# Cross-attention's borders: first queries ahead of the token transposes, folded weights between the first maxima, biases as bf16 rows

## The chip, the cores and the metric

The program runs on one core of one Trainium2 chip, as one launch. The metric is the device time of an execution in microseconds (us), the median over several runs. The profile is of one execution, and it has its own time.

## The reference, cut to what matters

The model holds x as 2 batches of 256 tokens with 256 channels and runs six layers, each added to x: a gelu layer against the context, a latent attention, a mixture-of-experts FFN ("MoE"), then a cross-attention, a holographic attention and a mixture attention. The change touches the cross-attention and what it hands to the holographic attention:

```python
def _L1_xattn_ref(values, keys, queries, mask, w_out, b_out):   # 16 heads of 16, 4096 keys
    energy = jnp.einsum('nqhd,nkhd->nhqk', q, k)
    energy = jnp.where(mask == 0, jnp.float32(-1e+20), energy)
    attn = jax.nn.softmax(energy / math.sqrt(EMBED), axis=3)
    out = jnp.einsum('nhql,nlhd->nqhd', attn, v).reshape(N, q_len, HEADS * HEAD_DIM)
    return out @ w_out.T + b_out

def _L1_attn_ref(x, Wq, bq, Wk, bk, Wv, bv):
    # unit_projection: fft, divided by its magnitude; bind/unbind: products of spectra
    query = unit_projection(jnp.einsum('bsd,ed->bse', x, Wq) + bq)
    keys = unit_projection(jnp.einsum('bsd,ed->bse', x, Wk) + bk)
    values = unit_projection(jnp.einsum('bsd,ed->bse', x, Wv) + bv)
    s = jnp.cumsum(bind(keys, values), axis=1)
    return unbind(s, query)

x = x + _L1_xattn_ref(ctx_1024, ctx_1024, _layernorm(x), mask, w_out, b_out)
x = x + _L1_attn_ref(_layernorm(x), Wq, bq, Wk, bk, Wv, bv)
```

## The kernel before, in words

Tokens lie on the partitions: x is four tiles (`NT`) of 128 tokens by 256 channels. A layernorm (`layernorm_T`) takes means and variances, makes the normalised tiles `xn` on VectorE (L121), transposes them with eight 128x128 transposes (`transpose_tokens`, L135), and two copies out of PSUM (L44 on VectorE, L46 on ScalarE) give `xnT`, channels on partitions.

**From the MoE.** Its results are gathered by eight indirect DMAs on POOL into the tiles `G` (L838), which VectorE adds to x (L807). Buffers opened after the MoE take over its memory, so their loads wait until the MoE is through with it.

**Cross-attention.** Its work is 32 units, one for each batch and head, with 8 steps each. A unit has its keys in one of five buffers `keys0` to `keys4`: four groups of 32 partitions, each with 16 rows of transposed context (`load_keys`, L868, SP) and 16 rows of ones (`set_ones`, L875; once for each buffer). Against the ones stand rows of the query tile `q0` that carry the negated maximum of each query, so that the energies come out with the maximum subtracted. Thus every unit is walked over twice: first step by step for maxima (`max_mms`: four f32 matmul records per step at L939 into `pm`, one VectorE maximum at L960), then for energies (`pe`), exponentials on ScalarE (L1055), masks on POOL (L1061) or VectorE, and the value products (`pav`). `place_mm` (L939) issues nearly all of these matmuls. A loop over T runs the maxima `LEAD` = 12 steps ahead of the energies. The stretch in which only maxima run is called the lead here. After eight maxima of a unit, `reduce_max_of` (mneg L967, mrows L969) and two transfers on SP, through `maxd` in HBM, bring the maxima into the query tile. `transfers` issues these and the later units' keys and queries in the order written.

Ahead of the lead come, in program order: loads of keys0 and keys1 with their ones, the output weights `wo` and bias `bo`, the layernorm "d", the queries of unit 1 by DMA, the ones of the three other key buffers, and the weights of the holographic attention (`wq`, `bq`, `dft`, `gates`, L914 to L918, SP). The queries of unit 0 don't go through DMA: `pad` (L926) puts the first 16 channels in place, sixteen matmul records at L930 place them, and L934 copies them to `q0`. After the eighth maximum, four VectorE additions put `bo` into x (L1164).

**Tail.** After the last step come 12 transposes of `wq` (L1178) with two copies (L1181), `combine` for the last unit (division by the sum, L1023 to L1028), the token transposes, and the output projection (L1189, added to x at L1192). Then the holographic weights are multiplied by the DFT matrix ("folded"): L1208 for the weights, L1216 for the biases, copies L1212 and L1219. The layernorm "e" follows. `spectrum` multiplies xnT by the folded weights `WD` (L1253), and adds the folded bias through a product of a tile of ones and `bD`, whose first row alone is not zero (L1257). Products and magnitudes on ScalarE, POOL and VectorE follow, and then the last layer.

Instructions on an engine run in its own order; `keep_in_program_order`, `issue_after` and manual dependencies fix parts of that order, and a scheduler decides the rest. DMAs are issued by SP, ACT and POOL, and a DMA also waits for the one before it on its lane.

Of the kernel before, what the change touches and what calls it, by code (L numbers as in the profile page):

```python
# [9 lines left out]
F32 = mybir.dt.float32  # L10
# [16 lines left out]
def tile_perceiver(ctx: ExitStack, tc: tile.TileContext, t):  # L27
# [67 lines left out]

    def layernorm_stats(mv, sm, tt):
        st = sm.tile([P, 6], F32, name="st", bufs=2)
        nc.vector.bn_stats(st, x[:, tt, :])
        nc.vector.bn_aggr(mv[:, tt, :], st)

    def layernorm_T(es, tag, scale_rows=None, mv=None, then=None, between=None, turn=None):
# [3 lines left out]
        pt, name = turn or (pool(es, f"lnp_{tag}", 2, PSUM), "ps_t")  # L105
# [14 lines left out]
        for tt in range(NT):  # L120
# [3 lines left out]
            )  # L124
        if between is not None:
            between()
        transpose_tokens(pt, xnT, xn, name)
# [419 lines left out]
    with ExitStack() as es:  # L547
# [246 lines left out]
        for n, u in enumerate(work):  # L794
# [8 lines left out]
            if u == ("s", 3):  # L803
                with tc.issue_after(turned_last[0].ins):
                    for tt in range(NT):
                        for i in range(2):
                            nc.vector.scalar_tensor_tensor(  # L807
# [44 lines left out]
    sig = wh.tile([P, 16], F32, name="sig")  # L852
    with ExitStack() as es:
# [19 lines left out]
        def set_ones(i, queues):  # L873
            for g in range(4):
                queues[g % len(queues)].dma_start(  # L875
# [4 lines left out]
        for u in range(2):  # L880
            list(load_keys(u))
            set_ones(u, (nc.sync, nc.gpsimd) if u == 0 else (nc.gpsimd,))
# [6 lines left out]
        QN = 5  # L889
        q0 = wk.tile([P, QN, S], F32, name="q0")  # L890
        with ExitStack() as es1:
            rooted = layernorm_T(es1, "d", scale_rows=anyq, mv=mvd, then=AF.Exp)

# [14 lines left out]
        with tc.issue_after(rooted.ins):  # L908
            nc.scalar.mul(q0[:, 1:, :], ones[:, 0:1].unsqueeze(2).to_broadcast([P, QN - 1, S]), 0.0)
        list(load_queries(1, (nc.sync, nc.scalar)))  # L910
        for i in range(2, KEYS):
            set_ones(i, (nc.gpsimd,))
        for j, n in enumerate("qkv"):
            nc.sync.dma_start(wq[:, j], t[f"W{n}T"].rearrange("(k p) e -> p k e", p=P))  # L914
            with nc.allow_non_contiguous_dma(reason="biases by channel"):
                nc.sync.dma_start(bq[:, j, :], t[f"L1_attn_b{n}"].rearrange("(k p) -> p k", p=P))
        nc.sync.dma_start(dft, t["dft"].rearrange("(k p) e -> p k e", p=P))
        nc.sync.dma_start(gates, t["L1_ffn_gates"].partition_broadcast(P))  # L918
# [3 lines left out]
        LEAD = 12  # L922
        mxs, max_rows = {}, {}


        nc.vector.tensor_copy(pad[:, :, 0:16], xn[:, 0:2, 0:16])  # L926
        pt = p_s.tile([P, 2, 512], F32, name="pm")[:, 0, 0:S]
        for qb in range(2):
            for g in range(4):
                nc.tensor.matmul(  # L930
                    pt[32 * g : 32 * g + 32, qb * P : (qb + 1) * P], lhsT=pad[:, qb, :], rhs=ident,
                    start=True, stop=True,
                )
        nc.vector.tensor_copy(q0[:, 0, :], pt)  # L934
# [99 lines left out]
        EB = 10  # L1034
        done = summed = divided = None
        n_steps = 8 * len(UNITS)
        def behind(later_one, one):

            tc.add_manual_dep(
                later_one.ins, one.ins.name,  # L1040
                mybir.DependencyInfo(mybir.DependencyClass.Sync, mybir.DependencyReason.DATA), reason="bank",
            )

# [21 lines left out]
        for T in range(-LEAD, n_steps + 4):  # L1065
# [7 lines left out]
            in_order = T < 4  # L1073
            tiles = 0 <= T < n_steps
# [84 lines left out]
            if i % 8 == 7 and i < n_steps:  # L1159
                last_max, max_rows[i // 8] = reduce_max_of(i // 8)  # L1160
                if i == 7:
                    with tc.issue_after(last_max.ins):
                        for tt in range(NT):
                            nc.vector.tensor_add(x[:, tt, :], x[:, tt, :], bo)  # L1164
# [17 lines left out]
        if done is not None:  # L1182
            combine(done)
# [425 lines left out]
```

## Time and profile before

| | |
|---|---|
| median of 3 runs | 956.43 us (956.0 to 960.83) |
| the profiled execution | 958.38 us, of which the profile's span is 956.7 us |
| mean TensorE clock granted, share of full | 0.959 |
| busy in the span | PE 894.9 us, PEld 533.6, DVE 590.0, ACT 405.9, POOL 512.3 |
| first gather of the MoE's results issued | 295.37 us |
| first max matmul / first energy | 318.14 / 338.51 us |
| last value product ends | 809.88 us |
| first DFT product of the tokens (L1253) | 828.27 us |
| keys of unit 0: issued by SP from | 305.20 us |
| weights of the holographic attention: issued by SP | 322.53 to 326.7 us |

PE is TensorE's matmul, PEld its weight load, DVE VectorE, ACT ScalarE, POOL GpSimd, SP SyncE. Times in the trace count from the span's start. An f32 matmul appears as several records. In the windows, the engine columns are busy us (and the number of instructions), then follow the granted clock, the share of the DMA engines' time and GB/s. In the chain, a line is a start, a duration, and the work that the end of the span depends on at that time.

### The profile page before, as it was taken

The page shows a single profiled execution, that of the slowest core. Times are in us where ns is not written, and L with a number is a line of the kernel's source. Part 1 is how long each engine was busy: PE and PEld are TensorE (multiplying, and loading weights), DVE is VectorE, ACT ScalarE, POOL GpSimd, SP SyncE. Part 2 cuts the span into 40 slices and gives each one's busy share as a digit, 9 for nine tenths or more (in the row PEclk, how much of TensorE's full clock was granted, in tenths as well). Part 3 has the DMA queues.
Part 4 walks back from the last instruction along what each step waited for, and adds up shares of the span by engine and source line. Part 5 has one row for each costly group of instructions (what it writes and reads, how often), then busy time and mean ns, then how long its engine had stood idle before and what let it go on. Part 6 is the DMA issues. An engine that isn't in the chain of part 4 may idle for free.

```text
span 956.7 us, 19287 instructions
## 1 busy us (share of the span) xinstructions
PE 894.9 (94%) x7170; PEld 533.6 (56%) x7170; DVE 590.0 (62%) x1154; ACT 405.9 (42%) x805; POOL 512.3 (54%) x521
## 2 busy tenths in 40 slices
PE   6999988789997789999999999999999999978997
PEld 5888855456664344555555445455555545754455
DVE  3434449442223778878888888888888874385342
ACT  2111137412221146666666666666666665321111
POOL 7322110010104268888888888888888886023830
PEclk9999999799999589999999999999999999987997
DMA  9865600356874610110110100101001000800000
GB/s 310 263 216 183 202 12 1 111 169 249 274 262 105 128 27 18 30 27 19 30 25 22 28 24 25 28 19 30 27 19 30 17 2 17 172 1 0 1 5 17
DMA packets 62513, 75.18 MB, mean 79 GB/s; under 512 B 21164, under 2 KB 49280, under 8 KB 62416
## 3 DMA queue, kind: packets, MB, share of 16 engines
q1 hardware_dynamic: 51240, 58.21, 20.1%
q10 hardware_dynamic: 8824, 10.40, 3.4%
q0 software_dynamic: 2352, 5.30, 2.3%
q8 instruction: 59, 0.97, 0.4%
q14 instruction: 38, 0.31, 0.1%
HBM read 68.79 MB, written 3.05 MB: 75 GB/s over the span
## 4 chain that ended last, share of the span: by engine, by line
PE 70%; DVE 4%; POOL 1%; issue 1%; ACT 1%; DMA 1%; ACTq 0%; DVEq 0%; POOLq 0%; SPq 0%
PE pe L939 22%; PE pav L939 15%; PE pm L939 11%; PE pp L1446 4%; PE py L630 3%; PE ga L605 2%; PE ua L605 2%; PE pa L1536 1%; DVE junk L960 1%; PE gb L605 1%; POOL G L838 1%; PE pp L1507 1%; PE pT L619 1%; PE pf L1253 1%; PE pf L1341 1%
## 5 line engine op out<-in xcount | busy, mean ns | idle before, releaser
L1061 POOL TENSOR_TENSOR e<-e,maskM 128x512 int32<-128x512 int32 x317 | 396.9, 1274 | 92.0 <-ACT e L1055 80.9
L1055 ACT ACTIVATE e<-pe 128x512 f32<-128x512 f32 x512 | 282.1, 596 | 198.4 <-PE pe L939 117.3
L960 DVE CUSTOM_DVE_ANT_1 junk<-pm,maskN 128x1024 f32<-128x1024 f32 x256 | 311.4, 1216 | 81.1 <-PE pm L939 79.3
L939 PE MATMUL pe<-q,keys 32*128 32x256 f32 x2048 | 292.7, 402 | 5.0 <-DVE mx L960 4.8
L939 PE MATMUL pm<-keys,q 32*128 32x512 f32 x1024 | 292.0, 660 | 1.5 <-DVE mx L960 0.9
L939 PEld LDWEIGHTS pe<-q,keys 32*128 32x128 f32 x2048 | 176.1, 185 | 98.1 <-SPq L1126 54.1
L939 PE MATMUL pav<-e,V 128*32 128x256 f32 x2048 | 163.6, 391 | 0.0
L939 PEld LDWEIGHTS pav<-e,V 128*32 128x32 f32 x2048 | 41.4, 108 | 85.6 <-issue 63.6
L939 PEld LDWEIGHTS pm<-keys,q 32*128 32x128 f32 x1024 | 79.7, 188 | 9.2 <-DVE mx L960 7.7
L1110 DVE SCALAR_TENSOR_TENSOR e<-e,maskM 128x512 f32<-128x512 f32 x67 | 70.4, 1051 | 11.9 <-ACT e L1055 11.9
L389 PE MATMUL ph<-xnT,ct 128*128 128x256 f32 x256 | 62.4, 389 | 1.5 <-ACT xnT L46 1.5
L363 PE MATMUL acc<-cn,g 128*128 128x256 f32 x256 | 60.5, 380 | 0.0
L218 POOL COPY V<-cn 128x256 f32<-128x256 f32 x64 | 26.1, 456 | 61.5 <-DMA cn<-in_ctx 53.1
L394 ACT ACTIVATE g<-ph 128x512 f32<-128x512 f32 x32 | 19.1, 597 | 91.7 <-PE ph L389 68.9
L389 PEld LDWEIGHTS ph<-xnT,ct 128*128 128x128 f32 x256 | 49.9, 196 | 9.0 <-ACT xnT L46 1.9
L363 PEld LDWEIGHTS acc<-cn,g 128*128 128x128 f32 x256 | 48.5, 190 | 7.1 <-ACT g L394 0.6
L939 PE MATMUL pe<-maskA,identb 128*128 128x512 bf16 x128 | 50.1, 391 | 0.1
L1446 PE MATMUL pp<-proj,xnT 128*128 128x512 f32 x96 | 46.4, 642 | 0.0
L636 POOL DMA_INDIRECT xg<-xnd,slot_token x9 | 8.6, 959 | 67.3 <-PE px L645 45.6
L939 PEld LDWEIGHTS <-identb 128*128 128x128 bf16 x128 | 12.2, 96 | 52.9 <-issue 52.9
L630 PE MATMUL py<-wd,hT 128*128 128x256 f32 x156 | 38.6, 389 | 1.3 <-ACT hT L621 1.3
L1460 POOL TENSOR_TENSOR pw<-pw 128x512 f32<-128x512 f32 (+2 forms) x33 | 27.5, 834 | 23.0 <-DVE pw L1451 21.3
(392 smaller groups left out, 868.5 us busy)
## 6 DMA issues: line engine op xcount, KB each, us to landing
ct<-in_ctxT SPq DMA_DIRECT2D x8, 1024.0 KB
cn<-in_ctx SPq DMA_DIRECT2D x8, 1024.0 KB
keys<-in_ctxT SPq DMA_DIRECT2D x128, 64.0 KB
wg<-in_L_ffn_we_gate SPq DMA_DIRECT2D x9, 688.0 KB
wu<-in_L_ffn_we_up SPq DMA_DIRECT2D x9, 688.0 KB
wd<-in_L_ffn_we_down SPq DMA_DIRECT2D x9, 640.0 KB
mi<-in_mask ACTq DMA_DIRECT2D x16, 256.0 KB
mi<-in_maskT ACTq DMA_DIRECT2D x16, 256.0 KB
```

What stands on the lines that cost most here:

```text
L218: nc.gpsimd.tensor_copy(Vh[:, n0 + j, :, 0:16], cn[:, j, :].rearrange("p (h w) -> p h w", w=16))
L363: nc.tensor.matmul(acc[e][qb], lhsT=g[:, j, qb * P : (qb + 1) * P], rhs=cn[:, fc % 8 + j, :], start=(fc + j == 0), stop=(fc + j == NKC - 1),)
L389: nc.tensor.matmul(ph[:, j, :], lhsT=ct[:, k, f0 : f0 + P], rhs=xnT[:, k, e * D : (e + 1) * D], start=(k == 0), stop=(k == 1),)
L605: nc.tensor.matmul(out[:, 0:n], lhsT=xT[k], rhs=m[:, k, f0 : f0 + n], start=(k == 0), stop=(k == 1))
L630: nc.tensor.matmul(py, lhsT=hT[0:m, c, :], rhs=w[2][0:m, c, :], start=(c == 0), stop=(c == NC6 - 1))
L939: mm = nc.tensor.matmul(*args, **kw)
L960: nc.vector.tensor_tensor_reduce(out=junk, in0=pm, in1=view, scale=1.0, scalar=-3.0e38, op0=ALU.add, op1=ALU.max, accum_out=mxs[u][:, qb, ...
L1055: nc.scalar.activation(e.rearrange("p j q -> p (j q)"), pe, AF.Exp, scale=1.0 / 16.0)
L1061: nc.gpsimd.tensor_tensor(ei, ei, maskM[:, KEPT[kt] : KEPT[kt] + 2, :], ALU.mult)
L1110: mul = nc.vector.scalar_tensor_tensor(e, e, 3.0e38, maskM[:, KEPT[kt] : KEPT[kt] + 2, :], op0=ALU.min, op1=ALU.mult)
L1446: nc.tensor.matmul(pp[:, hf * 512 : (hf + 1) * 512], lhsT=xnT[:, k, tt * P : (tt + 1) * P], rhs=proj[:, j, k, hf * 512 : (hf + 1) * 512], ...
L1460: nc.gpsimd.tensor_tensor(pw[:, 0:n], pw[:, 0:n], pw[:, n : 2 * n], ALU.add)
```

## The change

The loads of `wq`, `bq`, `dft` and `gates` move on SP from behind the keys to ahead of them. The loads of keys0 and keys1 and their ones now wait for the last use of `G` (`g_last`). In the layernorm "d" the pad copy follows the second normalised tile, and the first queries' matmuls precede the token transposes; of these, the first half precedes the first maxima, and the second half stands between the maxima of steps 1 and 2. Both halves are evacuated by ScalarE. The transposes of `wq` stand between the maxima at steps 3 to 5, the folding at steps 6 to 8, and that of the biases at step 9, where POOL splits them into three bf16 rows of a tile `BD`. The folded weights overwrite `wq`. `bo` is added to x on POOL. `LEAD` is 11. In the tail the weight transposes, the folding, and a second `combine` of the last unit are gone. The bias product in `spectrum` is one bf16 matmul of `pick` (which selects three rows) and `BD`.

```diff
         tc.keep_in_program_order(nc.scalar.activation(ready, eps, func))
+    def behind(later_one, one):
+        tc.add_manual_dep(
+            later_one.ins, one.ins.name,
+            mybir.DependencyInfo(mybir.DependencyClass.Sync, mybir.DependencyReason.DATA), reason="order",
+        )
...
-    def layernorm_T(es, tag, scale_rows=None, mv=None, then=None, between=None, turn=None):
+    def layernorm_T(es, tag, scale_rows=None, mv=None, then=None, between=None, turn=None, half_way=None):
         sm = pool(es, f"ln_{tag}", 1)
-        pt, name = turn or (pool(es, f"lnp_{tag}", 2, PSUM), "ps_t")
+        if half_way is None:
+            pt, name = turn or (pool(es, f"lnp_{tag}", 2, PSUM), "ps_t")
...
                 xn[:, tt, :], x[:, tt, :], mv[:, tt, 0:1], rstd[:, tt : tt + 1],
                 op0=ALU.subtract, op1=ALU.mult,
             )
+            if tt == 1 and half_way is not None:
+                half_way()
         if between is not None:
             between()
-        transpose_tokens(pt, xnT, xn, name)
+        if half_way is None:
+            transpose_tokens(pt, xnT, xn, name)
         return rooted
...
                 with tc.issue_after(turned_last[0].ins):
                     for tt in range(NT):
                         for i in range(2):
-                            nc.vector.scalar_tensor_tensor(
+                            g_last = nc.vector.scalar_tensor_tensor(
                                 x[:, tt, :], G[tt, i], cw[:, i, tt : tt + 1], x[:, tt, :], op0=ALU.mult, op1=ALU.add
                             )
                         if tt < 3:
     dft = wh.tile([P, 2, D], F32, name="dft")
     gates = wh.tile([P, 16], F32, name="gates")
     sig = wh.tile([P, 16], F32, name="sig")
+    for j, n in enumerate("qkv"):
+        tc.keep_in_program_order(nc.sync.dma_start(wq[:, j], t[f"W{n}T"].rearrange("(k p) e -> p k e", p=P)))
+        with nc.allow_non_contiguous_dma(reason="biases by channel"):
+            tc.keep_in_program_order(nc.sync.dma_start(bq[:, j, :], t[f"L1_attn_b{n}"].rearrange("(k p) -> p k", p=P)))
+    tc.keep_in_program_order(nc.sync.dma_start(dft, t["dft"].rearrange("(k p) e -> p k e", p=P)))
+    tc.keep_in_program_order(nc.sync.dma_start(gates, t["L1_ffn_gates"].partition_broadcast(P)))
+    BD = wh.tile([P, D], BF16, name="BD")
+    nc.gpsimd.memset(BD, 0.0)
+    pick = wh.tile([P, 3, P], BF16, name="pick")
...
         def set_ones(i, queues):
             for g in range(4):
-                queues[g % len(queues)].dma_start(
+                yield queues[g % len(queues)].dma_start(
                     kbuf[i][32 * g + 16 : 32 * g + 32, :],
                     onesd.rearrange("a b -> (a b)").unsqueeze(0).to_broadcast([16, 1024]),
                 )
         for u in range(2):
-            list(load_keys(u))
-            set_ones(u, (nc.sync, nc.gpsimd) if u == 0 else (nc.gpsimd,))
+            for transfer in load_keys(u):
+                behind(transfer, g_last)
+            for transfer in set_ones(u, (nc.sync, nc.gpsimd) if u == 0 else (nc.gpsimd,)):
+                behind(transfer, g_last)
         wo = wk.tile([P, 2, D], F32, name="wo")
         nc.sync.dma_start(wo, t["w_outT"].rearrange("(k p) c -> p k c", p=P))
         bo = wk.tile([P, D], F32, name="bo")
         QN = 5
+        EB = 10
         q0 = wk.tile([P, QN, S], F32, name="q0")
-        with ExitStack() as es1:
-            rooted = layernorm_T(es1, "d", scale_rows=anyq, mv=mvd, then=AF.Exp)
         def load_queries(u, queues, groups=range(4)):
...
-        with tc.issue_after(rooted.ins):
-            nc.scalar.mul(q0[:, 1:, :], ones[:, 0:1].unsqueeze(2).to_broadcast([P, QN - 1, S]), 0.0)
-        list(load_queries(1, (nc.sync, nc.scalar)))
-        for i in range(2, KEYS):
-            set_ones(i, (nc.gpsimd,))
-        for j, n in enumerate("qkv"):
-            nc.sync.dma_start(wq[:, j], t[f"W{n}T"].rearrange("(k p) e -> p k e", p=P))
-            with nc.allow_non_contiguous_dma(reason="biases by channel"):
-                nc.sync.dma_start(bq[:, j, :], t[f"L1_attn_b{n}"].rearrange("(k p) -> p k", p=P))
-        nc.sync.dma_start(dft, t["dft"].rearrange("(k p) e -> p k e", p=P))
-        nc.sync.dma_start(gates, t["L1_ffn_gates"].partition_broadcast(P))
         ahead = ExitStack()
         p_s = pool(ahead, "xa_0", 4, PSUM)
         ao = xn
-        LEAD = 12
+        LEAD = 11
         mxs, max_rows = {}, {}
-        nc.vector.tensor_copy(pad[:, :, 0:16], xn[:, 0:2, 0:16])
+        def padded():
+            nc.vector.tensor_copy(pad[:, :, 0:16], xn[:, 0:2, 0:16])
+        with ExitStack() as es1:
+            rooted = layernorm_T(es1, "d", scale_rows=anyq, mv=mvd, then=AF.Exp, half_way=padded)
+        with tc.issue_after(rooted.ins):
+            nc.scalar.mul(q0[:, 1:, :], ones[:, 0:1].unsqueeze(2).to_broadcast([P, QN - 1, S]), 0.0)
         pt = p_s.tile([P, 2, 512], F32, name="pm")[:, 0, 0:S]
         for qb in range(2):
             for g in range(4):
-                nc.tensor.matmul(
+                tc.keep_in_program_order(nc.tensor.matmul(
                     pt[32 * g : 32 * g + 32, qb * P : (qb + 1) * P], lhsT=pad[:, qb, :], rhs=ident,
                     start=True, stop=True,
-                )
+                ))
         nc.vector.tensor_copy(q0[:, 0, :], pt)
+        def half_tile():
+            return p_s.tile([P, 2, 512], F32, name="pm")[:, 0, :]
+        def turn_tokens(k):
+            ps = half_tile()
+            for tt in range(NT):
+                tc.keep_in_program_order(
+                    nc.tensor.transpose(ps[:, tt * P : (tt + 1) * P], xn[:, tt, k * P : (k + 1) * P], ident)
+                )
+            nc.scalar.copy(xnT[:, k, :], ps)
+        turn_tokens(0)
+        list(load_queries(1, (nc.sync, nc.scalar)))
+        for i in range(2, KEYS):
+            list(set_ones(i, (nc.gpsimd,)))
+        bqz = sm.tile([P, 2, S], F32, name="e", bufs=EB)[:, 0, :].rearrange("p (m c) -> p m c", m=2)
+        nc.gpsimd.memset(bqz, 0.0)
+        for n in range(3):
+            nc.gpsimd.tensor_copy(bqz[:, :, 32 * n : 32 * n + 3], bq.rearrange("p j m -> p m j"))
+        marks = wk.tile([P, 3], BF16, name="marks")
+        nc.gpsimd.tensor_tensor(marks, identb[:, 0:3], identb[:, 32:35], ALU.add)
+        nc.gpsimd.tensor_tensor(marks, marks, identb[:, 64:67], ALU.add)
+        nc.gpsimd.tensor_copy(pick, marks.unsqueeze(2).to_broadcast([P, 3, P]))
+        wqe = {}
+        def turn_weights(j):
+            ps = half_tile()
+            for m in range(2):
+                for k in range(2):
+                    at = (2 * m + k) * P
+                    tc.keep_in_program_order(
+                        nc.tensor.transpose(ps[:, at : at + P], wq[:, j, k, m * P : (m + 1) * P], ident)
+                    )
+            wqe[j] = sm.tile([P, 2, S], F32, name="e", bufs=EB)
+            nc.scalar.copy(wqe[j].rearrange("p m d -> p (m d)"), ps)
+        def fold(j):
+            ps = half_tile()
+            for k in range(2):
+                for m in range(2):
+                    place_mm(
+                        ps[:, k * D : (k + 1) * D], lhsT=wqe[j][:, m, k * P : (k + 1) * P], rhs=dft[:, m, :],
+                        start=(m == 0), stop=(m == 1),
+                    )
+            nc.scalar.copy(wq[:, j].rearrange("p k f -> p (k f)"), ps)
+        def fold_biases():
+            ps = half_tile()[:, 0:D]
+            for m in range(2):
+                place_mm(ps, lhsT=bqz[:, m, :], rhs=dft[:, m, :], start=(m == 0), stop=(m == 1))
+            ea = sm.tile([P, 2, S], F32, name="e", bufs=EB)
+            eb = sm.tile([P, 2, S], F32, name="e", bufs=EB)
+            parts = eb.rearrange("p a b -> p (a b)").bitcast(BF16).rearrange("p (n f) -> p n f", n=4)
+            nc.scalar.copy(ea[:, 0, :], ps)
+            for n in range(3):
+                nc.gpsimd.tensor_copy(parts[:, n, :], ea[:, n % 2, :])
+                nc.gpsimd.tensor_copy(BD[32 * n : 32 * n + 32, :], parts[32 * n : 32 * n + 32, n, :])
+                if n < 2:
+                    nc.gpsimd.tensor_tensor(ea[:, 1 - n % 2, :], ea[:, n % 2, :], parts[:, n, :], ALU.subtract)
+        between_maxima = {
+            2: lambda: turn_tokens(1),
+            3: lambda: turn_weights(1), 4: lambda: turn_weights(2), 5: lambda: turn_weights(0),
+            6: lambda: fold(1), 7: lambda: fold(2), 8: lambda: fold(0), 9: fold_biases,
+        }
         in_order = True
         held = []
         later, left = [], []
-        EB = 10
         done = summed = divided = None
         n_steps = 8 * len(UNITS)
-        def behind(later_one, one):
-            tc.add_manual_dep(
-                later_one.ins, one.ins.name,
-                mybir.DependencyInfo(mybir.DependencyClass.Sync, mybir.DependencyReason.DATA), reason="bank",
-            )
...
                 p_a = pool(es, "xa_a", 1, PSUM)
                 pa = p_a.tile([P, S], F32, name="pav")
             in_order = T < 4
+            if i in between_maxima:
+                between_maxima[i]()
...
             if i % 8 == 7 and i < n_steps:
                 last_max, max_rows[i // 8] = reduce_max_of(i // 8)
                 if i == 7:
-                    with tc.issue_after(last_max.ins):
-                        for tt in range(NT):
-                            nc.vector.tensor_add(x[:, tt, :], x[:, tt, :], bo)
+                    for tt in range(NT):
+                        nc.gpsimd.tensor_tensor(x[:, tt, :], x[:, tt, :], bo, ALU.add)
             if i <= n_steps + 1:
                 for transfer in transfers(i):
                     tc.keep_in_program_order(transfer)
-        wqe = wh.tile([P, 3, 2, D], F32, name="wqe")
-        wqf = wqe.rearrange("p j m d -> p (j m d)")
-        for n0 in (0, 8):
-            pm = p_s.tile([P, 2, 512], F32, name="pm")
-            pmf = pm.rearrange("p a b -> p (a b)")
-            n1 = min(12, n0 + 8)
-            for n in range(n0, n1):
-                j, m, k = n // 4, (n // 2) % 2, n % 2
-                nc.tensor.transpose(
-                    pmf[:, (n - n0) * P : (n - n0 + 1) * P], wq[:, j, k, m * P : (m + 1) * P], ident
-                )
-            nc.vector.tensor_copy(wqf[:, n0 * P : n1 * P], pmf[:, 0 : (n1 - n0) * P])
-        if done is not None:
-            combine(done)
         transpose_tokens(p_s, xnT, ao, "pm")
         for tt in range(NT):
             po = p_e.tile([P, D], F32, name="pe")
     wl = pool(last, "last_w", 1)
     mvf = wl.tile([P, NT, 2], F32, name="mvf")
-    WD = wl.tile([P, 3, 2, D], F32, name="WD")
-    bD = wl.tile([P, 3, D], F32, name="bD")
-    nc.gpsimd.memset(bD, 0.0)
-    with ExitStack() as es:
-        p_w = pool(es, "ha_w", 3, PSUM)
-        for j in (1, 2, 0):
-            pw = p_w.tile([P, 512], F32, name="pw")
-            for k in range(2):
-                for m in range(2):
-                    nc.tensor.matmul(
-                        pw[:, k * D : (k + 1) * D], lhsT=wqe[:, j, m, k * P : (k + 1) * P], rhs=dft[:, m, :],
-                        start=(m == 0), stop=(m == 1),
-                    )
-            nc.scalar.copy(WD[:, j].rearrange("p k f -> p (k f)"), pw)
-        for j in (1, 2, 0):
-            pw = p_w.tile([P, 512], F32, name="pw")
-            for m in range(2):
-                nc.tensor.matmul(
-                    pw[0:1, 0:D], lhsT=bq[:, j, m : m + 1], rhs=dft[:, m, :], start=(m == 0), stop=(m == 1)
-                )
-            nc.scalar.copy(bD[0:1, j, :], pw[0:1, 0:D])
     with ExitStack() as es:
         wk = pool(es, "ha", 1)
         wk2 = pool(es, "ha2", 2)
                 tt = 2 * b + tb
                 for k in range(2):
                     nc.tensor.matmul(
-                        pf[:, tb, :], lhsT=xnT[:, k, tt * P : (tt + 1) * P], rhs=WD[:, j, k, :],
+                        pf[:, tb, :], lhsT=xnT[:, k, tt * P : (tt + 1) * P], rhs=wq[:, j, k, :],
                         start=(k == 0), stop=False,
                     )
-                nc.tensor.matmul(pf[:, tb, :], lhsT=ones, rhs=bD[:, j, :], start=False, stop=True)
+                nc.tensor.matmul(pf[:, tb, :], lhsT=pick[:, j, :], rhs=BD, start=False, stop=True)
             return pf
...
```

More of the change, by code (lines that the diff above doesn't have):

```diff
@@ L929, in tile_perceiver @@
             for g in range(4):
-                nc.tensor.matmul(
+                tc.keep_in_program_order(nc.tensor.matmul(
                     pt[32 * g : 32 * g + 32, qb * P : (qb + 1) * P], lhsT=pad[:, qb, :], rhs=ident,
                     start=True, stop=True,
-                )
-        nc.vector.tensor_copy(q0[:, 0, :], pt)
+                ))
+        nc.vector.tensor_copy(q0[:, 0, :], pt)
+        def half_tile():
+            return p_s.tile([P, 2, 512], F32, name="pm")[:, 0, :]
```

## The prediction

> **What bounds the kernel now.** I read the page's chain first, then the windows of the cross-attention's loop, then the chain of waits around that loop's two ends, because the diff touches only those ends.
>
> ```profile
> PE 70%; DVE 4%; POOL 1%; issue 1%; ACT 1%; DMA 1%; ACTq 0%; DVEq 0%; POOLq 0%; SPq 0%
> 785.00:795.00 10.00, 10.00 (x97) 4.76 (x95) 4.28 (x7) 6.41 (x12) 6.84 (x7) 1.00 0.01 3
> ```
>
> TensorE carries the chain and is busy 10.00 of 10 us inside the loop, at full clock (the 1.00). The diff takes no matmul out of the loop, so the loop costs what it did. What can move is the lead (first maxima, ahead of the first energies), and the tail (from the last value product to the DFT products). The chain of waits, lead:
>
> ```profile
> 302.88 2.11 POOL G L838
> 305.29 0.60 POOL G L838
> 313.69 2.11 PE ps_t L135 x8
> 316.45 1.12 PE pm L930 x16
> 317.66 0.44 DVE q L934
> 318.14 5.20 PE pm L939 x20
> 331.57 0.16 DVE mneg L967
> 331.74 0.33 DVE x L1164
> 332.22 0.98 DVE x L1164 x3
> 338.51 0.79 PE pe L939
> ```
>
> See that the first queries (L930) stand behind the eight token transposes, that DVE maxima set the pace from 323 to 338, and that four additions of the bias `bo` sit among them. From the first max matmul (318.14) to the first energy (338.51) are 20.4 us. Windows of 2 us (busy PE, PEld, DVE, ACT, POOL; then clock, DMA share, GB/s):
>
> ```profile
> 320.00:322.00 2.00, 2.00 (x14) 1.05 (x8) 1.54 (x3) 0.00 (x0) 0.00 (x0) 0.50 0.37 47
> 324.00:326.00 2.00, 1.23 (x6) 0.30 (x4) 1.86 (x4) 0.00 (x0) 0.00 (x0) 1.00 0.84 219
> 328.00:330.00 2.00, 2.00 (x10) 0.63 (x5) 1.86 (x3) 0.00 (x0) 0.00 (x0) 0.50 0.76 192
> ```
>
> The lead runs mostly at half clock, and TensorE has holes as soon as the clock is full. The tail's chain:
>
> ```profile
> 811.49 1.14 DVE wqe L1181
> 818.13 5.18 PE pw L1208 x24
> 823.31 2.70 PE pw L1216 x12
> 826.03 0.37 ACT bD L1219
> 826.45 1.11 PE ps_t L135 x8
> 829.40 0.43 PE pf L1257 x2
> ```
>
> Folding the weights is 5.18 + 2.70 + 0.37 us on the chain, and each bias product 0.43.
>
> **The change, part by part.**
>
> *Tail.* Gone are the 12 weight transposes (L1178), their two DVE copies (L1181), the 24 + 12 folding records, and the second `combine` of the last unit. On the chain now: last value product 809.88, transposes .81, combine, wqe 1.14, then output projection, ending 818.13. Without L1178 (0.81), without the part of the wqe copy beyond the combine (1.14 + .04), and with the token copies free sooner (about .4), it ends at about 815.7: -2.4. Next late is the layernorm: xn began 820.26, so 817.9 now; in the following layernorm, where nothing covers it, xn at 864.23 precedes the first matmul at 866.92, so 2.7 us. The DFT products begin at about 820.6 instead of 828.27: -7.7 in all (5.3 beyond the 2.4). In the products, eight groups carry a 0.43 f32 bias; as one bf16 record it is about .14 (the bf16 128x512 mask product of the page takes 391 ns, 256 columns half of that at most; bounds .1 and .22). Eight times .29 = -2.3, all on the chain to 838.9; behind it the POOL and DVE steps shift along unchanged. Tail: -10.0. With the folding gone TensorE is idle for about 2.6 us before the products, which may lose it its clock; the window 812 to 814 had PE busy 1.14 of 2 and stayed at 1.00, while the idle stretch 848 to 852.8 ended in a half clock. Bounds 0 and +2.5 (the products' 8 x .86 partly at half rate); I take +0.9. Tail: **-9.1**.
>
> *Keys behind the weights.* SP now issues the eight loads (wq, bq, dft, gates; in before at 322.5 to 326.7, .51 each, so 4.1 us) ahead of the keys, and the first wq waits for the last use of G, as does every load of keys0 and keys1, on SP and on POOL. Without 0.5 MB of keys under it the eighth gather should land in its median of 3.2 us rather than 5.0, so G is used up at about 308.7 and the loads run to about 313. On POOL the memset of BD and the wait for G now stand ahead of keys0's and keys1's six ones (306.4 before) and of `bo`, which nobody needs before 331. Behind the weights on SP: four keys0 loads, two of its ones, keys1, `wo`, the unit-1 queries, keys2. The loads compete with POOL's ones, whose landing took 3.5 / 5.0 / 6.2 us (least, median, most), at 127 to 152 GB/s in 312 to 320; the weights alone moved at 219 to 247. 1.03 MB + 0.4 MB of ones give 6 to 9 us. keys0's ones wait on their DMA lane for dft, so they are issued at about 318 to 320 and land 2.5 later: first max matmul at 320.5 to 322.5, against 318.14. Bounds: 318 (keys land with the queries) and 326 (contention as in the worst ones). I take 322: **+3.9**. In before the queries came last (L934 ends 318.09); now they are ready at about 314 (no transposes ahead: -2.1, G sooner: -1.6, half the xn: about -.5) and then wait, so moving them ahead buys nothing unless the keys are early.
>
> *Lead.* Away from DVE: one max of twelve (LEAD 11), 1.37, and the bo additions, 0.33 + 0.15 + 0.98 = 1.46; they go to POOL, idle at that time (0.00 in the windows), so cost nothing; were POOL late, the first mask products would wait. Added on TensorE, by the tail's rows: four token transposes, 12 weight transposes, folds 5.18, bias folds .9 (a third of 2.70). A 4-matmul max tile is .87 warm, 1.7 cold; four transposes .44 warm (0.88 for six or eight seen), 1.04 cold (2.11 for eight). The evacuations (nine ACT copies of .58) lie on an ACT at 0.00 busy; the POOL splitting of biases on an idle POOL. With the first 5 us cold: three tiles 5.1 + transposes 1.0; three steps bound by DVE 3 x 1.37 = 4.1; three folds 3 x (.87 + 1.73) = 7.8; biases step 1.8; last step 1.4; fill and the last max 1.6. Sum 22.8 against 20.4: **+2.4**. Bounds: fully warm 21; fully cold 11 x 1.7 + 1.0 + 3.1 + 10.4 + 1.8 + 1.5 = 36.5.
>
> Here the trace has to be weighed against the Trainium skill, TensorE: Matmul & The Clock Gate, section Part 1: The HAM clock gate: full clock comes after one busy window of about 3.4 us. The rows above agree once (busy to 322, full clock at 322 to 324) and disagree once: 328 to 332 is busy 2.00 of 2, yet the clock stays 0.50 to the end of the lead. By the rule the lead warms within 3.4 to 6.8 us and stays so, 22.8; by the 328 row it could be 36.5, and the whole sum +9.6 instead of -4.0. The same page, section Part 4: PE-mode transpose, says transposes do not count as busy in the same way, which speaks against warming by the turned weights. I side with the rule because the new lead has few holes: the stretch that lost the clock was 1.23 of 2 busy, the new steps 6 to 9 are bound by TensorE.
>
> *Start of the loop.* In before the loop's first 4.8 us (338.5 to 343.3) ran at half clock, 2.4 us lost. Entering warm returns up to that: **-1.5** (bounds 0 and -2.4).
>
> *LEAD 11.* The queries with the row maxima of the next unit are issued 4.1 us ahead of its first energy, worst 3.5, and land 1.9 later: 2.2 of slack, worst 1.6. One step less takes 1.8. So the slack is about .4, and the worst three of 31 units late by up to .2: **+0.3**; bounds 0 and +6.
>
> Sum: 3.9 + 2.4 - 1.5 + 0.3 - 9.1 = -4.0. The profiled execution took 958.38 (span 956.7 and 1.7 around it), 1.95 above the median 956.43. So 954.4 profiled, **952.4** as a median.
>
> **Rivals.** *A, keys are not late.* If dft lands by 316 (weights at the 219 to 247 GB/s), keys0 follows by 318 to 319, the lead is warm and no longer than before: -4 from the sum above for the keys' part, -1.5 for the lead: 947. For: the keys no longer share the queues with gathers. Against: POOL's ones start at the same moment and slowed everything in 312 to 320.
>
> *B, slower: the lead at half clock.* Folding sits in the only stretch of the region where the clock was 0.50, whereas in the tail it ran at 1.00. Price: 36.5 - 22.8 = 13.7, and the 1.5 of the warm start: -4.0 + 15.2 = +11 and 967 if all of it is cold, about 962 if 60%. It decides for slower by 0.5% when the lead grows by over 9.7 us, i.e. with over half of that stretch at half clock. For: the 328 row. Against: dense work.
>
> *C, the row maxima come late at each unit.* If LEAD 11 leaves nothing of the slack, 31 borders at 0.2 give +6: 958.5. Against: 2.2 measured, 1.8 taken.
>
> **How the numbers follow.** Forecast 0.50 (947 to 958), A 0.23, B 0.19, C 0.08. What a measurement of this kernel can tell is 0.5%, 4.8 us: faster below 951.7, slower above 961.2. The forecast lies just above that border: of its 0.50, .23 faster, .24 same, .03 slower. A: .22 faster, .01 same. B: .03 same, .16 slower. C: .07 same, .01 slower. Together 0.45, 0.35, 0.20. The range 944 to 963 leaves out the coldest part of B and keys at 326.
>
> **What would show it.** In the new profile: first max matmul at 320.5 to 322.5 with the ones of keys0 as its releaser (before 319: A); 22 to 24 us from there to the first energy, with the clock at 1.00 in the fold steps (35: B); DFT products 9 to 10 us after the last value product ends, instead of 18.4; bias records below .25. I am wrong in kind if TensorE waits on q from maxd at unit borders, or the loop's 10 us windows change.

## The result, and the profile after

The changed kernel takes 1257.88 us (median of 4 runs, 1255.22 to 1258.53), before took 958.63 in the same comparison (4 runs, 956.0 to 961.14): a ratio of 1.3117, with a 95% interval of 1.3066 to 1.3167. The profiled execution has a span of 1253.5 us against 956.7.

The chain's shares on the page of after:

```profile
PE 76%; issue 2%; DVE 2%; DMA 1%; POOL 1%; ACT 0%; ACTq 0%; POOLq 0%; DVEq 0%; SPq 0%
```

The chain is TensorE's as before, with a larger share. Two windows of after, inside the loop:

```profile
400.00:410.00 10.00, 10.00 (x43) 4.22 (x41) 3.16 (x5) 2.76 (x5) 2.53 (x3) 0.50 0.02 5
750.00:760.00 10.00, 10.00 (x78) 4.93 (x74) 4.96 (x10) 4.40 (x8) 5.76 (x6) 1.00 0.06 14
```

TensorE is still busy 10.00 of 10 us, and this is what makes the row easy to misread. The telling column is the count. The same windows of before:

```profile
400.00:410.00 10.00, 10.00 (x122) 5.14 (x114) 7.81 (x15) 6.42 (x13) 8.82 (x8) 1.00 0.07 17
750.00:760.00 10.00, 10.00 (x126) 5.08 (x118) 7.84 (x15) 6.35 (x13) 8.91 (x8) 1.00 0.06 16
```

At full clock 78 matmuls run where 126 did. For 181 us (353.33 to 534.24) the clock is at half as well, and only 43 run. "Busy" is the time in which at least one matmul is in flight, and says nothing of how many are in flight together. The timeline of one step shows it. Before:

```profile
603.88 0.48 PE L939 MATMUL pe<-q,keys 32*128 32x256 f32 x2
603.90 0.70 PE L939 MATMUL pm<-keys,q 32*128 32x512 f32 x2
604.20 0.60 PE L939 MATMUL pe<-q,keys 32*128 32x256 f32 x4
604.43 0.59 PE L939 MATMUL pm<-keys,q 32*128 32x512 f32 x2
```

After, at the same clock:

```profile
600.27 0.70 PE L1029 MATMUL pe<-q,keys 32*128 32x256 f32 x4
600.80 1.02 PE L1029 MATMUL pm<-keys,q 32*128 32x512 f32 x4
601.66 0.60 PE L1029 MATMUL pe<-q,keys 32*128 32x256 f32 x4
602.19 0.64 PE L1029 MATMUL pav<-e,V 128*32 128x256 f32 x8
```

In before, two energies (`pe`) and two maxima (`pm`) start within 0.02 us of each other and run side by side. In after the maxima begin 0.53 us behind the energies, and the next energies wait for them in turn: three stretches one behind the other, and behind them the value products. A step takes 2.49 to 2.81 us instead of 1.64 to 1.96. A unit takes 21.2 us instead of 14.4 at full clock, and 40.0 at half clock.

The reason lies in lines that the diff doesn't show. Energies and maxima use 32 of the array's 128 rows each, one of four row groups. In step s the first energies take row group 2 (s even) or 0 (s odd), by `first_bank`; those of its second half, one of them left over from the step before, take group 3 or 1, by `second_bank`. The maxima of step i take groups 0 and 1 (i even) or 2 and 3 (i odd), by `gp = s % 2`. With i = T + 12 the parities agree, and the maxima stand on the two groups that the step's energies leave free. With i = T + 11 they fall on the very two groups that the energies use. The Trainium skill, TensorEngine Tiling (Array Packing), in Tiling Modes, Key Properties, says of such row tiles: "Different tiles can execute LdWeights and Matmul in parallel". The timelines above agree, and show the reverse: matmuls on the same tile queue up.

The lead begins, in after's timeline (SP issues two ones of keys0; the first max matmul waits for keys' ones):

```profile
316.82 0.78 SPq L896 DMA_DIRECT2D keys<-onesd x2
321.84 2.42 PE L1029 MATMUL pm<-keys,q 32*128 32x512 f32 x8 [10.77 <-DMA keys<-onesd]
```

It goes on in the chain of waits:

```profile
324.26 1.04 PE pm L962 x4
325.31 2.01 PE pm L1029 x4
327.31 1.05 PE pm L989 x4
351.92 0.45 PE pe L1029
```

The first max matmul comes at 321.84 (before 318.14), the first energy at 351.92 (before 338.51). The clock stayed at half until 339.68. The maxima lose their overlap here too: two steps' maxima, on all four row groups, take 2.42 us together, while those of one step between two sets of transposes (L962, L989) take 2.01. The tail, from the timeline of after:

```profile
1121.38 1.94 PE L147 MATMUL ps_t<-ident,xn 128*128 128x128 f32 x8 [2.69 <-DVE xn L130]
1124.05 2.08 PE L1297 MATMUL pf<-wq,xnT 128*128 128x256 f32 x4 [0.73 <-ACT xnT L46]
1125.92 0.42 PE L1301 MATMUL pf<-BD,pick 128*128 128x256 bf16 x1
1128.97 0.27 PE L1301 MATMUL pf<-BD,pick 128*128 128x256 bf16 x1
```

The first DFT product starts 10.75 us after the last value product ends (1113.30), where before took 18.39. The 1.94 for eight transposes (1.11 in before's chain), and the 0.42 that becomes 0.27, show that the tail does lose its clock for a while.

The whole difference of the spans, by the same marks in both traces: first energy +13.4; first energy of unit 0 to that of unit 31 (453.1 in before, 743.1 in after) +290.0; from there to the last value product 0.0; end of the last value product to the start of the last squares of keys and values on ScalarE (29.05 and 20.86) -8.2; the rest +1.6. The sum is 296.8.

### The profile page after: what moved, and what is told of

Read it like the earlier page. It is cut to its first block, busy times and chain, and to the rows that moved or that the text cites. A ratio compares the mean times of both kernels' runs of the same rounds, so it can differ in the third digit from the quotient of the medians.

```text
span 1253.5 us, 19261 instructions
## 1 busy us (share of the span) xinstructions
PE 1184.6 (95%) x7146; PEld 650.4 (52%) x7146; DVE 574.4 (46%) x1144; ACT 432.0 (34%) x807; POOL 528.3 (42%) x541
## 4 chain that ended last, share of the span: by engine, by line
PE 76%; issue 2%; DVE 2%; DMA 1%; POOL 1%; ACT 0%; ACTq 0%; POOLq 0%; DVEq 0%; SPq 0%
PE pe L1029 28%; PE pm L1029 21%; PE pav L1029 13%; PE pp L1490 3%; PE py L642 2%; PE ga L617 1%; PE ua L617 1%; PE pa L1580 1%; PE gb L617 1%; DMA bo<-in_L_xattn_b_out 1%; PE pp L1551 1%; POOL G L850 1%; PE pT L631 1%; PE pf L1385 0%; DVE R L1573 0%
## 5 line engine op out<-in xcount | busy, mean ns | idle before, releaser
L1143 POOL TENSOR_TENSOR e<-e,maskM 128x512 int32<-128x512 int32 x318 | 404.8, 1273 | 354.4 <-ACT e L1137 353.1
L1137 ACT ACTIVATE e<-pe 128x512 f32<-128x512 f32 x512 | 304.6, 597 | 443.3 <-PE pe L1029 439.2
L1029 PE MATMUL pe<-q,keys 32*128 32x256 f32 x2048 | 367.4, 438 | 2.9 <-DVE mx L1050 2.8
L1029 PEld LDWEIGHTS pe<-q,keys 32*128 32x128 f32 x2048 | 193.3, 203 | 232.8 <-issue 168.2
L1029 PE MATMUL pm<-keys,q 32*128 32x512 f32 x1024 | 298.5, 667 | 10.8 <-DMA keys<-onesd 10.8
L1029 PE MATMUL pav<-e,V 128*32 128x256 f32 x2048 | 178.7, 423 | 0.0
L1029 PEld LDWEIGHTS pm<-keys,q 32*128 32x128 f32 x1024 | 108.9, 209 | 30.4 <-issue 13.6
L1194 DVE SCALAR_TENSOR_TENSOR e<-e,maskM 128x512 f32<-128x512 f32 x66 | 48.9, 740 | 15.5 <-ACT e L1137 15.3
L1029 PE MATMUL pe<-maskA,identb 128*128 128x512 bf16 x128 | 54.0, 422 | 0.0
L1504 POOL TENSOR_TENSOR pw<-pw 128x512 f32<-128x512 f32 (+2 forms) x33 | 27.6, 837 | 23.0 <-DVE pw L1495 21.2
```

What stands on the lines that cost most here:

```text
L1029: mm = nc.tensor.matmul(*args, **kw)
L1137: nc.scalar.activation(e.rearrange("p j q -> p (j q)"), pe, AF.Exp, scale=1.0 / 16.0)
L1143: nc.gpsimd.tensor_tensor(ei, ei, maskM[:, KEPT[kt] : KEPT[kt] + 2, :], ALU.mult)
L1194: mul = nc.vector.scalar_tensor_tensor(e, e, 3.0e38, maskM[:, KEPT[kt] : KEPT[kt] + 2, :], op0=ALU.min, op1=ALU.mult)
L1504: nc.gpsimd.tensor_tensor(pw[:, 0:n], pw[:, 0:n], pw[:, n : 2 * n], ALU.add)
```

## The experiments

Three theories for the 290 us of the loop: P, the pairing of row groups; S, the distance, since LEAD 11 leaves the row maxima less time; H, the lead's folding leaves TensorE at half clock. Four kernels tell them apart.

**e1_after_lead12.** After with the even distance.

```diff
-        LEAD = 11
+        LEAD = 12
```

> After with LEAD = 12 instead of 11, nothing else. Theory P (pairing of row groups): with an odd LEAD the step's maxima and its energies read the same 32-row groups of the array and can't run side by side; with 12 they are apart again, a unit takes 14.4 us as before (21.2 in after at full clock), and the loop gets back its 290 us. What is left is the lead (first energy 351.92 in after against 338.51, and one more maximum, so +14.8) and the tail (-8.2): span about 963. Theory S (distance): LEAD 11 makes the row maxima late; LEAD 12 cures that too, same number. Theory H (clock): the lead's folding leaves TensorE at half clock well into the loop; then the first units run at half clock here too, 4 units at 25 to 29 us: span 1000 or more.

Measured: 967.35 us (4 runs), ratio to before 1.0110 (1.0089 to 1.0131), span 963.9. A unit takes 14.4 us, and 121 matmuls run in 10 us:

```profile
750.00:760.00 10.00, 10.00 (x121) 4.82 (x113) 7.76 (x16) 6.15 (x12) 8.60 (x8) 1.00 0.10 25
```

The loop has its 290 us back (453.5 from unit 0 to unit 31). H falls: with the same folding in the lead the clock rose for good at 353.67, 6.4 us into the loop.

**e3_after_lead11_flipped.** After, with LEAD 11, and the groups of the maxima exchanged.

```diff
-            qb, c, gp = s // 4, (s // 2) % 2, s % 2
+            qb, c, gp = s // 4, (s // 2) % 2, 1 - s % 2
```

> After with its LEAD of 11, but each maximum takes the other two row groups of its step (gp = 1 - s % 2; the same eight maxima in another order). P: groups of maxima and energies are apart again, a unit takes 14.4 us, span about 962. S: the distance is still 11, so as slow as after, 1253. H: 1000 or more, since the lead is that of after.

Measured: 967.81 us (4 runs), ratio 1.0112 (1.0081 to 1.0143). This parts P from S: the distance is still 11, and the loop is as fast as with 12 (452.9 us from unit 0 to unit 31). S falls.

**e2_before_lead11 and e4_before_flipped.** The same two edits, each alone in before.

> Before with LEAD = 11 instead of 12, nothing else of the change. P: a unit takes 21.2 us at full clock instead of 14.4, 31 units give +211: at least 1165, and about 1245 if the clock also stays at half for the first four units as in after. S: lateness of the row maxima only, 0.2 us per unit: about 963. H: without the folding in the lead the clock rises at about 343 as in before: no more than 965.

> Before with its LEAD of 12, but each maximum takes the other two row groups of its step (gp = 1 - s % 2). P: groups collide though the distance is 12: a unit takes 21.2 us or more, at least 1165. S: no change, 957. H: no change, 957.

Measured, one execution each: 1320.41 and 1251.57 us. So either edit, alone in before, brings the loss of 290 us or more, with nothing else of the change. (In e2 the clock stayed at half for longer than in after, see below.) A window of e3:

```profile
750.00:760.00 10.00, 10.00 (x117) 5.02 (x113) 8.26 (x14) 6.37 (x13) 8.87 (x8) 1.00 0.15 37
```

The same window of e4:

```profile
750.00:760.00 10.00, 10.00 (x80) 4.69 (x78) 5.60 (x11) 4.67 (x8) 6.37 (x5) 1.00 0.03 7
```

In both, TensorE is busy all the time; only the count tells them apart. P holds in all four.

**g1_after_dense: the half clock.** At full clock the collision costs 31 x 6.8 = 211 us of the 290. The other 79 are half clock. In after the clock rose at 534.24, just behind the first products of `combine_four` in the loop (L1090, L1098):

```profile
531.25 1.08 PE L1090 MATMUL pm<-av,stack 128*32 128x256 f32 x8
532.10 1.08 PE L1029 MATMUL pav<-e,V 128*32 128x256 f32 x8
533.12 0.61 PE L1029 MATMUL pe<-maskA,identb 128*128 128x512 bf16 x1
533.52 0.63 PE L1098 MATMUL pm<-ident,avs 128*128 128x128 f32 x2
```

The clock changes on a grid of 3.41 us in these traces, and all four fall into the grid's stretch that ended at 534.24. Products of this height are nothing new there: value products (`pav`) and mask products come in ordinary steps too. New is how many of them stand in one stretch. In e4 the rise at 520.01 also ended a stretch that held the same four rows (516.78 to 519.68). In e2 the first such four rows (513.51 to 516.41) lay across the grid's edge at 514.34 and nothing rose; the next rose the clock at 678.18. To test whether denser work raises the clock, g1 puts 16 full-array records, which nobody reads, into after:

```diff
+            if T == 3:
+                dense = p_s.tile([P, 2, 512], F32, name="pm")[:, 0, 0:D]
+                for n in range(8):
+                    place_mm(dense, lhsT=wq[:, 1, 0, 0:P], rhs=dft[:, 0, :], start=True, stop=True)
```

> After as it is (LEAD 11), with 16 more matmul records over the full 128x128 array at the loop's step T = 3, whose result nobody reads; they take 7.2 us at half clock. If the loop with colliding row groups is too thin for the clock to rise by itself (in after it rose at 534.24, in the one window that held the products of combine_four), the clock rises within 7 us of them and the first four units take 21.2 us instead of 40.0: span about 1253 - 75 + 7 = 1185. If something else holds the clock down, the span is 1260.

Measured: 1180.55 us (one execution), span 1178.8, 74.7 less than after. The records ran from 362.04 to 368.43, and the clock rose at 367.47 and stayed. Its windows:

```profile
362.00:372.00 10.00, 10.00 (x45) 6.86 (x45) 2.47 (x5) 1.94 (x4) 1.27 (x1) 0.73 0.01 3
372.00:382.00 10.00, 10.00 (x82) 4.71 (x80) 5.92 (x11) 4.63 (x8) 6.36 (x5) 1.00 0.02 6
```

So denser work ends the half clock, and with the pairing mended (e1, e3) the loop does not stay in it. The long half clock thus follows from the collision.

What is dense enough can be estimated from the records of the eleven traces. Take each matmul record with its share of the 128x128 array (32*128 and 128*32 are a quarter each) and the time of its columns: 0.43 us for 512 f32 columns at full clock, as two pairs of maxima pass between 600.80 and 601.66 above, twice that at half clock, and, as an assumption, half of it for bf16. Of 485 grid stretches at half clock, 96 were followed by full clock. These had filled at least 0.74 of the array, the 389 others at most 0.78. The colliding loop at half clock filled 0.43 to 0.64 in after, e2 and e4, and 0.70 in e2's cut stretch; the stretches with `combine_four` that raised the clock filled 0.81 to 0.82, g1's 1.0. Once the clock was up, the colliding loop of after kept it at 0.48 to 0.63; no stretch that lost the clock had filled more than 0.35. What the chip itself counts is not shown.

**What is left: the lead.** With the pairing mended, the change is still 1.1% slower. The first energy of e1 comes at 347.31, 8.8 us later than in before: 4.3 by the late first max matmul (322.43, with `q0` ready at 311.1), 4.5 by a longer lead (24.9 against 20.4). **f1_keys_first** puts the eight loads behind keys1 on SP:

```diff
         for u in range(2):
...
+        for j, n in enumerate("qkv"):
+            tc.keep_in_program_order(nc.sync.dma_start(wq[:, j], t[f"W{n}T"].rearrange("(k p) e -> p k e", p=P)))
...
         wo = wk.tile([P, 2, D], F32, name="wo")
```

> After with LEAD 12 (as in e1), and on SP the loads of wq, bq, dft and gates stand behind keys0, its ones and keys1 instead of ahead of them. If the late keys are what holds the first maximum (e1: first max matmul 322.43 while q0 is ready at 311.1), the first max matmul comes at about 312 to 313 and everything behind it about 10 us sooner, less what the lead waits for the weights: span 953 to 957. If the ones on POOL and the traffic of 308 to 320 hold it whatever the order on SP, it comes at 318 or later, and the span is 960 or more.

Measured: 963.78 us (6 runs), ratio 1.0065 (1.0033 to 1.0098). The first max matmul came at 314.79, 7.6 us sooner than in e1, but the first energy only at 352.95, and the span (962.9) missed the 953 to 957. SP's waits in f1 (what waited, for what: us in total, times, longest) show a new one:

```profile
SPq L902 <- DMA q<-xnT: 8.0, 1, 8.0
```

And so does its chain of waits:

```profile
314.50 7.26 DMA q<-xnT
323.35 3.18 DMA wq<-in_WkT
326.66 1.09 PE pm L989 x4
```

SP stood 8.0 us before the first weight load until a DMA of unit 1's queries had landed. The weight transposes stood ahead of the next maxima in TensorE's order, and so the maxima waited for the weights. The delay had only changed its carrier.

**f2_fold_under_layernorm.** f1, with the folds behind the output projection.

```diff
-            6: lambda: fold(1), 7: lambda: fold(2), 8: lambda: fold(0), 9: fold_biases,
+            6: fold_biases,
...
             nc.vector.tensor_add(x[:, tt, :], po, x[:, tt, :])
+        for j in (1, 2, 0):
+            fold(j)
```

> f1, and the folding products (not the weight transposes, and not those of the biases, which move up to step 6) are issued behind the output projection, beside the layernorm that follows it. In e1 TensorE idles there for some 5 us (output projection to the layernorm's transposes) and the clock falls to half for 6.8 us. If the lead is bound by TensorE in its fold steps, the lead shortens by 3 to 8 us and the tail grows by no more than 1: span 946 to 951. If the folds hide in the lead at no cost, the span is that of f1 or 1 to 3 longer.

Measured: 965.04 us (4 runs), ratio 1.0090 (1.0060 to 1.0120). That is no gain over f1 that the runs resolve, and the span (962.2) missed the 946 to 951. The trace has the first energy 6 us earlier (346.94), but only 3.3 of them are left at the last squares and 0.7 at the end; the same wait (8.1 us) held the weights. It did show that the tail keeps its gain with the folds in it: 21.2 us from the last value product to the last squares, against 29.05 in before and 20.86 in after.

**h1_before_keys_wait.** Before, with only the keys' wait for the last use of G.

```diff
-            list(load_keys(u))
-            set_ones(u, (nc.sync, nc.gpsimd) if u == 0 else (nc.gpsimd,))
+            for transfer in load_keys(u):
+                behind(transfer, g_last)
+            for transfer in set_ones(u, (nc.sync, nc.gpsimd) if u == 0 else (nc.gpsimd,)):
+                behind(transfer, g_last)
```

> Before, with the loads of keys0 and keys1 and their ones waiting for the last use of G, as in after, and nothing else of the change. If the keys' traffic delayed the last gather (G used up at 310.83 in before, 305.4 in after), G is used up at about 305.5, the layernorm and the first queries follow 5 us sooner, and the first max matmul at about 313: span 951 to 953. If the keys then land too late, the gain is lost: span 955 to 957.

Measured: 957.53 us (12 runs), ratio 0.9997 (0.9979 to 1.0014). In its trace G is used up at 306.50, the first max matmul comes at 313.76 and the first energy at 334.63, 3.9 us sooner than in before's. The timed runs don't show these 3.9 us: a difference between two single traces is weaker evidence than 12 runs, and where the gain goes stayed open.

**i1_lead_free.** After with LEAD 12, keys first, the weights loaded where before has them; the weight transposes behind the last maximum of the lead, the folding of biases and weights behind the output projection.

```diff
-            3: lambda: turn_weights(1), 4: lambda: turn_weights(2), 5: lambda: turn_weights(0),
-            6: fold_biases,
...
             if i < n_steps:
                 max_mms(i)
+            if T == -1:
+                turn_weights()
...
             nc.vector.tensor_add(x[:, tt, :], po, x[:, tt, :])
+        fold_biases()
         for j in (1, 2, 0):
             fold(j)
```

> After with LEAD 12, keys first on SP, and the holographic weights loaded where before loads them; the weight transposes stand behind the last maximum of the lead, where TensorE idles for about 6 us in before (332.7 to 338.5); the foldings of biases and weights are issued behind the output projection, beside the layernorm. If the lead was the only place where after's other steps lost their gain, the first max matmul comes at about 313.5 and the first energy at about 335 (h1: 313.76 and 334.63), the tail from the last value product to the last squares takes 21 us (f2: 21.2, before 29.0): span 946 to 949, ratio about 0.99. If the transposes behind the last maximum delay the first energies, or POOL's splitting of the biases delays the first bias product, one or two us of that are lost: 948 to 952.

Measured: 952.19 us (7 runs; before 958.00 in the same comparison), ratio 0.9931 (0.9906 to 0.9956): 0.7% faster than before, and far faster than after. The span was 948.1, 8.6 below that of before, of which the tail gives 7.1. First max matmul 313.68, first energy 335.21, last value product to last squares 22.0 us (29.05 in before), about as expected; the lead still ran at half clock from 324.28 to 341.35. Its tail, in the timeline:

```profile
813.82 5.34 PE L1030 MATMUL pm<-dft,wqk 128*128 128x256 f32 x24
815.24 2.64 DVE L130 TENSOR_SCALAR xn<-x,mv,rstd 128x256 f32<-128x256 f32 x4
819.83 1.10 PE L147 MATMUL ps_t<-ident,xn 128*128 128x128 f32 x8 [0.68 <-ACT wq L1006]
```

The folds run beside the normalisation, the eight transposes behind them take 1.10 (the clock was kept; 1.94 in after), and the first DFT product comes 13.9 us after the last value product instead of 18.4.

## Why the prediction was wrong

**The step that failed** is in what bounds the kernel: "The diff takes no matmul out of the loop, so the loop costs what it did." The first half is true. The second took the loop's cost to be a sum over its matmuls, while it was set by which of them run together: the same matmuls took 743.1 us instead of 453.1 from unit 0 to unit 31. LEAD was costed twice, as one maximum less and as slack of the row maxima, never as what sets the partner of each energy. The windows of before gave the hint: energies and maxima have 585 us of busy time by the page's groups (292.7 and 292.0), the value products 163.6, and the loop with its lead lasted 492: 1.52 times the stretch. Records overlap at their ends even in a queue, so that after, too, has 845 us in 791, or 1.07. But 1.52 cannot fit unless whole matmuls run side by side, and then the question is what lets them. The prediction named a change of the loop's windows as being "wrong in kind", and that it was.

**Rival C** had the right edit (LEAD 11) and the wrong mechanism. The slack was in fact enough: e3 has LEAD 11 and no loss in the loop (452.9 us, before 453.1).

**Keys behind the weights** was right: 322 was taken, 321.84 measured, with the ones of keys0 as releaser, behind `dft` on their lane (SP stood 1.3 us for it). So Rival A, keys by 318 to 319, falls. That the number fits is in part luck, as two errors cancelled: G was used up at 305.40, not 308.7, so the ones were issued at 316.8, not 318 to 320; but the first max matmul followed 5.0 us behind their issue, where 2.5 was taken for the landing.

**The lead** was mis-sized: 22.8 predicted, 30.1 measured (321.84 to 351.92). The term at fault is "the first 5 us cold". The clock came only at 339.68, 18 us after the first max matmul. In e1, with the same order of work, it came at 326.37, and the lead was 24.9, of which the twelfth maximum is 1.4. So the sum was good for an early clock, and Rival B was half true. The rule weighed there, of the Trainium skill (TensorE: Matmul & The Clock Gate, Part 1: The HAM clock gate), that the full clock comes after one busy window, does not hold for these streams: after was busy 10.00 of 10 at 0.50 for 181 us. The row of 328 to 332, which the prediction set aside, was the better guide. By the estimate above, the stretch before e1's rise filled 0.74 of the array and the one at the same place in after (322.61 to 326.03) 0.70, so both lay near the limit; the next three of after, with transposes between single steps' maxima, filled 0.53 to 0.56, and the one that ended at 339.68, with folds, 0.92. That such a small difference decided between e1 and after is argued from this estimate, not tested.

**The start of the loop** (-1.5) failed: TensorE idles at the lead's end (349.15 to 351.92 in after, while VectorE finishes), and the clock fell back at 353.33, in e1 at 346.85. The first unit of e1 took 16.2 us, that of before 15.8.

**The tail** was right: -8.2 measured, -9.1 predicted, the first DFT product after 10.75 us for 9 to 10 predicted. A half-spectrum goes from 1.30 to .98 us with the bf16 bias, .32 for the .29 taken. The clock was lost from 1121.33 to 1128.16, which costs about 2.7 us by the rows (.83 in the transposes, .95 in each of the first two groups), just over the upper bound of 2.5, where 0.9 was taken.

Without the loop the measured terms are +13.4 - 8.2 + 1.6 = +6.8. In e1, where the pairing is whole, the span is 7.2 above that of before (the medians are 10.8 apart).

## What to carry to other kernels

A constant that sets how far one stream of matmuls runs ahead of another also sets which of them meet; where they use a part of the array's rows, list the row groups of every matmul in one step before and after the edit. Read the count of matmuls in a window beside the busy time, and compare the sum of their durations with the stretch: if it is far above it (1.52 times here, 1.07 in a queue), overlap holds the time, and an edit that moves no matmul can still break it. Work that is taken off the tail has to be put where the engine waits for something else, as i1 does; put ahead of a first load or between steps at half clock it costs more than it saved.

## What the runs showed of the hardware

- Matmuls on different 32-row groups run side by side, on the same group one behind the other: 126 against 78 in 10 us at full clock, both with TensorE busy all the time.
- A busy TensorE need not get its full clock. With colliding 32-row matmuls it stayed at half for 181 us in after, and from the first energy for 184 us in e4 (336.03 to 520.01) and 345 in e2 (332.76 to 678.18). Denser stretches of the 3.41 us grid raised it: `combine_four` in three kernels and 6.4 us of spare products in g1. The same loop then kept it to its end.
- It is not the height of single products that counts: in before, maxima alone, 32 rows each but side by side, raised the clock at 322.80. By the estimate, the array was filled to at least 0.74 in the stretch before each rise.
- The same lead took its full clock at 326.37 in e1 and at 339.68 in after, so one profile does not give the clock of a stretch that is near the limit.
